# Selective scan: which engine makes the products with B, the first block's own order, and where five norms stand

## The chip, the cores and the metric

The kernel runs on one core of a Trainium2 chip. The metric is the device time of one execution in microseconds (us), as the median of several runs. A core has five engines that run their own queues in order and meet through semaphores: PE (TensorE, matrix products into PSUM), DVE (VectorE, elementwise work and scans), ACT (ScalarE, activation functions), POOL (GpSimd, elementwise work on SBUF alone here) and SP (SyncE, which issues the DMAs). PEld is PE's weight load.

## The reference

Four layers follow each other on two images of 128 channels and 64 x 64 pixels: attention, snake convolutions, convolution steps and, last, a selective scan in four directions (rows forwards and backwards, columns forwards and backwards). The change is in the last alone. For each direction, over a sequence of 4096 positions:

```python
dt = jax.nn.softplus(dt @ W_dt.T + b_dt)
A = -jnp.exp(A_log)
dA = jnp.exp(dt[..., None] * A)
dBu = dt[..., None] * Bm[:, :, None, :] * xh[..., None]
...
h = dA_t * h + dBu_t            # at each step t, for 256 channels x 16 states
...
y = jnp.einsum('lbdn,bln->bld', hs, Cm)
y = y + xh * Dp
y = y * jax.nn.silu(z)
return y @ W_out.T
```

The input is normalized over its channels first (mean, variance, scale). B and C come from xh by a matrix product; xh is a short convolution of the input followed by silu, and z another product.

## The kernel before

Layer 3 is one function, `layer3`. It works on 64 blocks: two images, four directions each, eight blocks of 512 positions per direction. A block has 8 groups of 4 tiles: two halves of the channels (`hf`) times four groups of four states (`ng`). A tile is 128 partitions (32 channels times 4 states) by 512 positions in fp32, so a group's `db` is 128 x 2048 and a block has 32 tiles.

A group k goes through these steps, each on one engine:

- `weights` (PE): the four rows of B of the group are spread over the partitions into PSUM, tile `pbc`, by a product with a selector.
- `db_dve` (DVE): the first n tiles of `db` = `pbc` times dt*x, where n is `ND[hf][ng]`. dt and dt*x lie spread over partitions in SBUF (`dd4`, one for each half).
- `db_pool` (POOL): the other 4 - n tiles, from a copy of B's rows in SBUF that a DMA has broadcast (`copies(.., "b", ..)`).
- `expo` (ACT): `da` = exp(dt*A) for one tile into PSUM, issued two tiles ahead of the scan; `da` has three buffers.
- `scan` (DVE): one scan per tile, in place in `db`, with the last column of the block before (`hl`) as its start. The first block of a direction starts at zero.
- `keep` (ACT): saves the last column of the group into `hl`.
- `cmul` (POOL): `db` times C's rows, in place; it may begin only when keep has read `db`.
- `sums` (PE): folds the four states and adds up over the groups into `py`.
- `gate` (DVE), `project` (PE) and `finish` (ACT): times silu(z), the output projection on top of the running image, and the copy back into it.

The scan layer stands in a manual schedule: the order of the calls in the code is the order in each engine's queue. The loop runs over k; within it `slot` is k modulo 8 and i the block. At slot s the loop issues the scans of group k, then `db_dve(k + 1)`, `db_pool(k + 1)` and `cmul(k - 1)`, and beside them one eighth of the preparation of block i + 1: its x product (slot 0), dt (slots 1 and 2), softplus, sums and the spreading through DRAM (`spread`, `spread_store`, `spread_load`), z (slot 4), and in slots 5 to 7 the convolution of block i + 2 with its silu. `transfers` issues the DMAs: spread_load is 8 transfers of 256 KB for each half, and B's and C's rows come by four transfers of 64 KB for each group. Silu needs another table than exp and ln, so each silu has a table load ahead and one behind it.

In before, `ND` is ((4, 2, 1, 4), (1, 4, 1, 4)): DVE makes 21 of a block's 32 tiles, in eight instructions, and POOL makes 11 in four. The pool `wk`, which holds `db`, has four buffers. `finish(i - 1)` is issued at the start of slot 6, so ACT does it ahead of slot 6's exponentials.

The norm of a row (here a row is one block of 512 positions) is `ln_mean` (PE), `ln_less` (DVE), `ln_square` (ACT), `ln_var` (PE), `ln_log` and `ln_root` (ACT), `ln_scale` (POOL) and `ln_store` (ACT). The mean and the variance use `da`'s PSUM buffers. In before all eight rows of the first image are normalized ahead of the loop, in a software pipeline with the preparation of block 0 and of block 1's convolution; the second image's eight rows are normalized one per block in blocks 22 to 29 (`next_norm`), at slots 0, 1, 3, 4 and 6. `turn` writes the column-wise copy of the first image in blocks 0 to 3, two rows in each.

## Time and profile before

| what | us |
|---|---|
| median of 3 runs (lowest to highest) | 5898.72 (5897.96 to 5899.47) |
| the profiled execution | 5899.89 |
| its span, first to last instruction | 5898.1 |
| scan layer: first DMA to first scan | 2453.30 to 2523.34 |
| scan layer: first scan to last scan's end | 2523.34 to 5883.5 |
| scan layer: last scan's end to the end | 14.6 |

The granted PE clock was 0.887 over the span. The page gives busy times over the whole span, in which three other layers fill the first 2453 us; for the scan layer they say little. The prediction therefore cuts the span into stages. In its listings a line of the timeline has start, length, engine, source line, operation, output and inputs, shape, count, and in brackets the idle time of the engine just before it and what ended it. A line of the groups has busy time and mean ns of one behind the count, and then the idle time before those instructions. Busy times of one instruction and the next overlap by some 0.1 us[...].

### The profile page before, as it was taken

The numbers are of one execution on the slowest core, as the hardware profiler recorded it, in microseconds if no ns is written. First come the engines' busy times: TensorE is split into PE (matmuls) and PEld (weight loads), VectorE is DVE, ScalarE is ACT, GpSimd is POOL, SyncE is SP. The second block draws the span as 40 slices with busy tenths as digits, with TensorE's granted clock in tenths as the row PEclk, the third lists the DMA queues.
The fourth block names the chain that finished last, engine by engine and source line by source line (L and its number), as shares of the span: only waits on it lengthen the run. The fifth ranks groups of instructions, "written<-read, shape, count | busy, mean of one in ns | idle before, by whom it ended". The sixth has DMA issues, their size and how long they took to land.

```text
span 5898.1 us, 58825 instructions
## 1 busy us (share of the span) xinstructions
PE 4930.2 (84%) x19238; PEld 1735.4 (29%) x19238; DVE 4452.2 (75%) x4266; ACT 3816.1 (65%) x5499; POOL 3632.0 (62%) x1200
## 2 busy tenths in 40 slices
PE   7999999989978779877777787878777787777776
PEld 3333333334434334322222222222222222222221
DVE  5333333355124688589999999999999999999998
ACT  4888888840035511377777777777777777777775
POOL 5111111100010021089999999999999999999999
PEclk8999999999988889988888888888888888888887
DMA  5000001030056200056655556555655566555564
GB/s 155 19 19 19 19 19 33 1 59 1 4 112 109 64 11 0 20 131 146 143 133 135 130 140 145 128 131 141 151 134 134 129 139 146 139 132 134 137 148 104
DMA packets 345402, 558.75 MB, mean 95 GB/s; under 512 B 70480, under 2 KB 125280, under 8 KB 344000
## 3 DMA queue, kind: packets, MB, share of 16 engines
q1 hardware_dynamic: 341952, 551.37, 40.4%
q10 hardware_dynamic: 3136, 3.56, 0.2%
q8 instruction: 152, 2.49, 0.2%
q14 instruction: 162, 1.33, 0.1%
HBM read 465.59 MB, written 89.13 MB: 94 GB/s over the span
## 4 chain that ended last, share of the span: by engine, by line
PE 52%; DVE 27%; POOL 9%; issue 5%; DMA 4%; ACT 2%; SPq 1%; DVEq 0%; POOLq 0%; ACTq 0%
DVE db L1429 18%; PE ps L287 10%; PE acc L303 8%; DVE db L1404 7%; POOL db L1439 6%; PE pm L1294 6%; PE m L1052 6%; PE m L566 5%; PE py L1447 2%; PE pm L1359 2%; PE pm L1466 2%; PE pm L1464 2%; PE acd L812 2%; DMA dx<-dd 1%; POOL dd L1367 1%
## 5 line engine op out<-in xcount | busy, mean ns | idle before, releaser
L1439 POOL TENSOR_TENSOR db<-db,c 128x2048 f32<-128x2048 f32 x512 | 2313.4, 4535 | 92.3 <-ACT hl L1434 82.6
L1429 DVE TENSOR_TENSOR_SCAN db<-da,hl,db 128x512 f32<-128x512 f32 x1792 | 2166.1, 1266 | 69.1 <-ACT da L1420 21.1
L1420 ACT ACTIVATE da<-dd,am 128x512 f32<-128x512 f32 x2048 | 1398.0, 689 | 727.5 <-DVE db L1429 701.2
L293 ACT ACTIVATE e<-ps 128x1024 f16<-128x1024 f32 x1024 | 992.2, 1021 | 135.6 <-PE ps L287 123.9
L1388 PE MATMUL pbc<-bc,sel 64*128 64x512 f32 x512 | 288.3, 563 | 695.4 <-DVE db L1404 695.3
L1413 POOL TENSOR_TENSOR db<-b,dd 128x1536 f32<-128x1536 f32 (+1 forms) x256 | 811.5, 3170 | 9.0 <-PE py L1447 4.4
L1404 DVE TENSOR_TENSOR db<-pbc,dd 128x2048 f32<-128x2048 f32 (+2 forms) x512 | 785.3, 1534 | 0.6 <-PE pbc L1388 0.6
L314 DVE RECIPROCAL rec<-acc 32x512 f32<-32x512 f32 x64 | 214.9, 3358 | 640.4 <-PE acc L303 640.4
L321 POOL TENSOR_TENSOR parts<-parts 32x512 f32<-32x512 f32 x64 | 80.5, 1257 | 976.2 <-DVE parts L320 976.2
L1447 PE MATMUL py<-db,fold 128*32 128x512 f32 x4096 | 639.7, 701 | 39.8 <-POOL db L1439 38.4
L287 PE MATMUL ps<-q,k 32*128 32x512 f32 x4096 | 656.4, 643 | 3.6 <-DVE flag L250 2.8
L303 PE MATMUL acc<-e,v 128*128 128x512 f16 x2048 | 532.1, 382 | 0.0
L1388 PEld LDWEIGHTS pbc<-bc,sel 64*128 64x128 f32 x512 | 105.8, 207 | 1184.1 <-DVE db L1404 1070.4
L1052 PE MATMUL m<-v,u 128*128 128x512 f32 x864 | 379.7, 603 | 49.3 <-DVE v L1021 49.3
L1359 PE MATMUL pm<-dd,ident 128*128 128x512 f32 x512 | 365.3, 852 | 4.6 <-ACT dd L1352 4.4
L1429 DVE TENSOR_TENSOR_SCAN db<-da,db 128x512 f32<-128x512 f32 x256 | 294.8, 1206 | 30.4 <-ACT da L1420 22.5
L303 PEld LDWEIGHTS <-v 128*128 128x128 bf16 x2048 | 158.5, 97 | 510.6 <-issue 389.4
L287 PEld LDWEIGHTS ps<-q,k 32*128 32x128 f32 x4096 | 229.4, 184 | 228.4 <-issue 169.6
L566 PE MATMUL m<-comb,w 64*128 64x512 f32 (+4 forms) x1296 | 269.9, 575 | 0.0
L686 POOL TENSOR_SCALAR yt<-y 32x512 f32<-32x512 f32 x8 | 18.2, 2272 | 379.8 <-DVE y L677 379.4
L1052 PEld LDWEIGHTS m<-v,u 128*128 128x128 f32 x864 | 166.9, 194 | 262.1 <-issue 216.1
L1294 PE MATMUL pm<-xn,wcs 128*128 128x512 f32 x512 | 237.1, 606 | 3.0 <-ACT z L1312 2.6
(317 smaller groups left out, 5991.2 us busy)
## 6 DMA issues: line engine op xcount, KB each, us to landing
dd<-dx SPq DMA_DIRECT2D x1024, 256.0 KB, 6.8
dx<-dd SPq DMA_DIRECT2D x128, 512.0 KB, 3.3
c<-bx SPq DMA_DIRECT2D x1024, 64.0 KB, 2.2
b<-bx SPq DMA_DIRECT2D x768, 64.0 KB, 3.3
hats<-pos SPq DMA_DIRECT2D x136, 256.0 KB, 9.8
q<-qd SPq DMA_DIRECT2D x32, 512.0 KB, 7.5
w<-in_conv0T SPq DMA_DIRECT2D x18, 288.0 KB, 8.8
q<-in_x SPq DMA_DIRECT2D x8, 512.0 KB, 6.3
```

Source lines behind the costliest of these rows:

```text
L287: nc.tensor.matmul(ps[:, i, :], k4[h % 2][rows, kb // 4, :], q4[h % 2][rows, qb * BLK : (qb + 1) * BLK], start=True, stop=True,)
L293: nc.scalar.activation(e[:, :n, :], ps[:, :n, :], AF.Exp)
L303: nc.tensor.matmul(acc, v3[b][:, kb, h, :], e[:, i, :], start=(kb == 0), stop=(kb == NS - 1))
L566: yield lambda q=q, dy=dy, src=src, i0=i0, i1=i1: nc.tensor.matmul(m[:, i0 * NF : i1 * NF], w[half, dy, q, x, :], src, start=(dy == KC and ...
L1052: nc.tensor.matmul(m[x], weights[j][:, dy, x, :], v[j][b][:, x, r0 : r0 + RP, :].rearrange("p r i -> p (r i)"), start=(dy == 0), stop=(dy ...
L1294: nc.tensor.matmul(pu, wcs[:, hf, s, :], window(blk, sgn * s), start=(s == 0), stop=(s == 3))
L1404: nc.vector.tensor_tensor(x["db"][:, :n, :], x.pop("pb").unsqueeze(1).to_broadcast([P, n, BLK]), S[i]["d4", hf][:, 1, :n, :], ALU.mult)
L1413: nc.gpsimd.tensor_tensor(x["db"][:, n:, :], S[i]["b", ng].unsqueeze(1).to_broadcast([P, 4 - n, BLK]), S[i]["d4", hf][:, 1, n:, :], ALU.mult)
L1420: nc.scalar.activation(da, S[i]["d4", hf][:, 0, q, :], AF.Exp, scale=am[:, hf, q, ng : ng + 1])
L1429: nc.vector.tensor_tensor_scan(d1, d0, d1, 0.0 if first else hl[:, hf, ng, q, :], ALU.mult, ALU.add)
L1439: nc.gpsimd.tensor_mul(v, v, S[i]["c", ng].unsqueeze(1).to_broadcast([P, 4, BLK]))
L1447: nc.tensor.matmul(S[i]["y", hf][32 * q : 32 * q + 32, :], fold, G[k]["db"][:, q, :], start=False, stop=(ng == NNG - 1),)
```

## The change

- `ND` becomes ((4, 0, 1, 4), (4, 4, 0, 4)). DVE still makes 21 tiles and POOL 11, but two groups (1 of the first half, 2 of the second: slots 1 and 6) are POOL's alone, and only one is shared. For the two, `weights` has no product and `db_dve` no instruction. Group 0 needs no copy of B now.
- `wk` gets a fifth buffer, and POOL's product is issued for group k + 2, behind `cmul(k - 1)`, instead of for k + 1 ahead of it. B's copies are issued one slot earlier (`ahead` 4 instead of 3).
- `finish(i - 1)` moves from the start of slot 6 to just before its fourth tile.
- Ahead of the loop only three rows are normalized, and block 0's preparation is written out in an order of its own. Rows 3 to 7 are normalized in blocks 0 to 4, in other buffers (`xc` and `sq`), as the second image's are; `turn` runs in blocks 1 to 4.

```diff
@@ -1127,7 +1127,7 @@
     nc, tc = g.nc, g.tc
     NJ = 4
 
-    ND = ((4, 2, 1, 4), (1, 4, 1, 4))
+    ND = ((4, 0, 1, 4), (4, 4, 0, 4))
     NNG = N_STATE // NJ
     HB = 1
     HC = 3
@@ -1174,7 +1174,7 @@
                     nc.tensor.transpose(pw[:, s * P : (s + 1) * P], ws, g.ident)
                 nc.vector.tensor_copy(wcs[:, hf].rearrange("p s o -> p (s o)"), pw)
         d4 = ctx.enter_context(tc.tile_pool(name="l3d4", bufs=2))
-        wk = ctx.enter_context(tc.tile_pool(name="l3wk", bufs=4))
+        wk = ctx.enter_context(tc.tile_pool(name="l3wk", bufs=5))
         up = ctx.enter_context(tc.tile_pool(name="l3u", bufs=2))
         ck = ctx.enter_context(tc.tile_pool(name="l3ck", bufs=2))
 
@@ -1205,6 +1205,7 @@
         xn = a.tile([P, HW + 2 * HB, HW], F32, name="xn")
         xt = a.tile([P, L + 2 * HC], F32, name="xt")
         N = {}
+        NFIRST = 3
 
 
         def ln_tile():
@@ -1216,7 +1217,7 @@
             nc.tensor.matmul(N[k, "mean"], onesm, interior(g, b, k * RB, RB), start=True, stop=True)
 
         def ln_less(b, k):
-            if b == 0:
+            if b == 0 and k < NFIRST:
 
                 t = wk.tile([P, 4, BLK], F32, name="db")
                 N[k, "xc"], N[k, "sq"] = t[:, 0, :], t[:, 1, :]
@@ -1384,9 +1385,12 @@
         def weights(k):
 
             i, hf, ng = groups[k]
+            G[k] = {}
+            if ND[hf][ng] == 0:
+                return
             pb = psb.tile([P, BLK], F32, name="pbc")
             nc.tensor.matmul(pb, sel[:, ng].rearrange("p j c -> p (j c)"), S[i]["bc"], start=True, stop=True)
-            G[k] = {"pb": pb}
+            G[k]["pb"] = pb
 
         def copies(i, x, ng):
 
@@ -1397,22 +1401,28 @@
             for j in range(NJ):
                 nc.sync.dma_start(t[32 * j : 32 * j + 32], S[i]["bx"][r0 + j].partition_broadcast(32))
 
+        def db_tile(k):
+            if "db" not in G[k]:
+                G[k]["db"] = wk.tile([P, 4, BLK], F32, name="db")
+            return G[k]["db"]
+
         def db_dve(k):
             i, hf, ng = groups[k]
-            x, n = G[k], ND[hf][ng]
-            x["db"] = wk.tile([P, 4, BLK], F32, name="db")
-            nc.vector.tensor_tensor(
-                x["db"][:, :n, :], x.pop("pb").unsqueeze(1).to_broadcast([P, n, BLK]), S[i]["d4", hf][:, 1, :n, :], ALU.mult
-            )
+            n = ND[hf][ng]
+            if n:
+                nc.vector.tensor_tensor(
+                    db_tile(k)[:, :n, :], G[k].pop("pb").unsqueeze(1).to_broadcast([P, n, BLK]),
+                    S[i]["d4", hf][:, 1, :n, :], ALU.mult,
+                )
 
         def db_pool(k):
             i, hf, ng = groups[k]
-            x, n = G[k], ND[hf][ng]
-            if n == 4:
-                return
-            nc.gpsimd.tensor_tensor(
-                x["db"][:, n:, :], S[i]["b", ng].unsqueeze(1).to_broadcast([P, 4 - n, BLK]), S[i]["d4", hf][:, 1, n:, :], ALU.mult
-            )
+            n = ND[hf][ng]
+            if n < 4:
+                nc.gpsimd.tensor_tensor(
+                    db_tile(k)[:, n:, :], S[i]["b", ng].unsqueeze(1).to_broadcast([P, 4 - n, BLK]),
+                    S[i]["d4", hf][:, 1, n:, :], ALU.mult,
+                )
 
         def expo(k, q):
             i, hf, ng = groups[k]
@@ -1516,7 +1526,7 @@
                     spread_store(i, 1)
             if slot == 0 and i - 1 < NBK:
                 spread_load(i - 1, 1)
-            for x, ahead in (("b", 3), ("c", 1)):
+            for x, ahead in (("b", 4), ("c", 1)):
                 j, ng = divmod(8 * (i - 1) + slot + ahead, 8)
                 if ng < NNG and 0 < j < NBK:
                     copies(j, x, ng)
@@ -1548,6 +1558,8 @@
 
         def next_norm(i):
 
+            if i < NBLK - NFIRST:
+                return 0, NFIRST + i
             b, k = divmod(i, 4 * NBLK)
             k -= 4 * NBLK - 2 - NBLK
             return (b + 1, k) if b + 1 < NB and 0 <= k < NBLK else None
@@ -1560,41 +1572,62 @@
             nc.vector.memset(xt[:, HC + L :], 0.0)
             nc.vector.memset(xn[:, HB - 1, HW - HC :], 0.0)
             nc.vector.memset(xn[:, HB + HW, :HC], 0.0)
-
-            for t in range(NBLK + 2):
-                slot = t - 2
-                if slot == 6:
-                    for k in range(2):
-                        weights(k)
-                    db_dve(0)
-                    db_pool(0)
-                if slot >= 0:
-                    front_pe(0, slot)
-                    front_act(0, slot)
-                    front_pool(0, slot)
-                if slot == 1:
-                    bc_store(0)
-                elif slot in (3, 4):
-                    spread_store(0, slot - 3)
-                    if slot == 3:
-                        spread_load(0, 0)
-                        copies(0, "b", 0)
-                        copies(0, "c", 0)
-                if t < NBLK:
-                    for part in (ln_mean, ln_less, ln_square):
-                        part(0, t)
-                if 0 <= t - 1 < NBLK:
-                    for part in (ln_var, ln_log, ln_root, ln_scale, ln_store):
-                        part(0, t - 1)
-                if t == 1:
-                    begin(0)
-                    conv(0, 1)
-                    conv_silu(0)
-            for ng in range(1, NNG):
+            units = [(k, q) for k in range(len(groups)) for q in range(4)]
+            AHEAD = 2
+
+            for k in range(NFIRST):
+                ln_mean(0, k)
+            for k in range(NFIRST):
+                ln_less(0, k)
+            ln_square(0, 0)
+            ln_var(0, 0)
+            ln_log(0, 0)
+            ln_root(0, 0)
+            ln_scale(0, 0)
+            ln_square(0, 1)
+            ln_store(0, 0)
+            begin(0)
+            conv(0, 1)
+            ln_var(0, 1)
+            ln_log(0, 1)
+            ln_root(0, 1)
+            ln_scale(0, 1)
+            conv_silu(0)
+            front_pe(0, 0)
+            front_act(0, 0)
+            bc_store(0)
+            front_pe(0, 1)
+            front_act(0, 1)
+            ln_store(0, 1)
+            sum_parts(0, 0)
+            sum_copy(0, 0)
+            spread(0, 0)
+            spread_store(0, 0)
+            spread_load(0, 0)
+            softplus(0, 1)
+            front_pe(0, 3)
+            front_act(0, 3)
+            spread(0, 1)
+            spread_store(0, 1)
+            for ng in range(NNG):
                 copies(0, "b", ng)
                 copies(0, "c", ng)
-            units = [(k, q) for k in range(len(groups)) for q in range(4)]
-            AHEAD = 2
+            for k in range(2):
+                weights(k)
+            db_dve(0)
+            db_pool(0)
+            front_pe(0, 4)
+            front_act(0, 4)
+            front_pe(0, 5)
+            front_pe(0, 6)
+            ln_square(0, 2)
+            ln_var(0, 2)
+            ln_log(0, 2)
+            ln_root(0, 2)
+            ln_scale(0, 2)
+            ln_store(0, 2)
+            front_act(0, 7)
+            db_pool(1)
             for u in range(AHEAD):
                 expo(*units[u])
             for k in range(len(groups) + 7):
@@ -1606,9 +1639,9 @@
                 if k + 2 < len(groups):
                     weights(k + 2)
                 norm = next_norm(i)
-                if slot == 6 and 1 <= i <= NBK:
-                    finish(i - 1)
                 for q in range(4):
+                    if slot == 6 and q == 3 and 1 <= i <= NBK:
+                        finish(i - 1)
                     if norm and slot == 3 and q == 3:
                         ln_log(*norm)
                     if 4 * k + q + AHEAD < len(units):
@@ -1630,9 +1663,10 @@
                     ln_less(*norm)
                 if more:
                     db_dve(k + 1)
-                    db_pool(k + 1)
                 if ended:
                     cmul(k - 1)
+                if k + 2 < len(groups):
+                    db_pool(k + 2)
 
                 if slot == 5 and 0 <= k - 2 < len(groups):
                     sums(k - 2)
@@ -1652,9 +1686,9 @@
                         ln_store(*norm)
                 if live:
 
-                    if slot == 6 and i % (4 * NBLK) < NBLK // 2:
+                    if slot == 6 and 0 < i % (4 * NBLK) <= NBLK // 2:
                         for n in range(2):
-                            turn(blocks[i][0], 2 * (i % (4 * NBLK)) + n)
+                            turn(blocks[i][0], 2 * (i % (4 * NBLK) - 1) + n)
 
                 if slot != 5 and 0 <= k - 2 < len(groups):
                     sums(k - 2)
```

## The prediction

> **What bounds the kernel now.** I read the busy time by stage first, then groups by shape in the selective scan, then one block's timeline on each engine, then every idle gap of VectorE (DVE). By stage (span, busy and count of PE, weight loads, DVE, ACT, POOL, then clock and DMA), the scan layer's start and its 64-block loop:
>
> ```profile
> 2453.30:2523.30 70.00, 54.13 (x107) 19.94 (x108) 15.78 (x36) 42.07 (x61) 17.98 (x12) 0.87 0.35 88
> 2578.00:5883.50 3305.50, 2568.46 (x7717) 783.18 (x7717) 3217.53 (x2650) 2387.67 (x3920) 3213.61 (x887) 0.84 0.58 136
> ```
>
> In the loop DVE (3217.53) and GpSimd, POOL (3213.61), are each busy 97% of 3305.5 us; in the 70 us before it DVE does almost nothing. The change touches only these two stages. Shapes in the loop:
>
> ```profile
> L1429 DVE TENSOR_TENSOR_SCAN db<-da,hl,db 128x512 f32<-128x512 f32 x1789 | 2162.6, 1266 | 69.0 <-ACT da L1420 21.1 <-DVE db L1404 0.9 <-ACT hl L1434 0.5
> L1404 DVE TENSOR_TENSOR db<-pbc,dd 128x2048 f32<-128x2048 f32 x251 | 569.1, 2267 | 0.0
> L1404 DVE TENSOR_TENSOR db<-pbc,dd 128x512 f32<-128x512 f32 x189 | 126.0, 666 | 0.0
> ...
> L1439 POOL TENSOR_TENSOR db<-db,c 128x2048 f32<-128x2048 f32 x504 | 2277.3, 4535 | 83.2 <-ACT hl L1434 73.4 <-DMA dd<-dx 9.5
> L1413 POOL TENSOR_TENSOR db<-b,dd 128x1536 f32<-128x1536 f32 x189 | 650.2, 3440 | 8.4 <-PE py L1447 3.7 <-DMA c<-bx 3.0 <-POOL db L1439 0.9
> ```
>
> Busy times of neighbours overlap, so I take pitches, start to next start, from a block's timeline (start, length, engine, line):
>
> ```profile
> 5218.03 0.67 DVE L1404 TENSOR_TENSOR db<-pbc,dd 128x512 f32<-128x512 f32 x1
> 5218.80 2.46 DVE L1429 TENSOR_TENSOR_SCAN db<-da,hl,db 128x512 f32<-128x512 f32 x2
> 5221.17 0.67 DVE L1456 TENSOR_TENSOR gt<-py,z 128x512 f32<-128x512 f32 x1
> 5221.75 2.45 DVE L1429 TENSOR_TENSOR_SCAN db<-da,hl,db 128x512 f32<-128x512 f32 x2
> 5224.12 2.27 DVE L1404 TENSOR_TENSOR db<-pbc,dd 128x2048 f32<-128x2048 f32 x1
> 5226.49 4.81 DVE L1429 TENSOR_TENSOR_SCAN db<-da,hl,db 128x512 f32<-128x512 f32 x4
> ...
> 5209.32 4.53 POOL L1439 TENSOR_TENSOR db<-db,c 128x2048 f32<-128x2048 f32 x1 [1.14 <-ACT hl L1434]
> 5213.80 3.43 POOL L1413 TENSOR_TENSOR db<-b,dd 128x1536 f32<-128x1536 f32 x1
> 5217.19 9.04 POOL L1439 TENSOR_TENSOR db<-db,c 128x2048 f32<-128x2048 f32 x2
> ```
>
> A product with B of n tiles costs DVE 0.77 (n=1), 1.31 (n=2) or 2.37 us (n=4) until the scan that waits for it starts; a scan 1.18; a gate 0.58. One block is 32 x 1.18 + 4 x 2.37 + 1.31 + 3 x 0.77 + 2 x 0.58 = 52.05 with no idle, and undisturbed blocks repeat every 52.08. POOL needs 8 x 4.49 + 3 x 3.40 + 2.33 + 2 x 1.23 = 50.9 and waits some 1.1. So DVE bounds, POOL is 1.2 us behind it. Gaps then add to the time; the two kinds, DVE's gap and ACT's wait that makes it:
>
> ```profile
> 3702.61 2.46 DVE L1429 TENSOR_TENSOR_SCAN db<-da,hl,db 128x512 f32<-128x512 f32 x2 [1.99 <-ACT da L1420]
> 3700.77 0.57 ACT L1340 CAST bc<-pm 32x512 fp32r<-32x512 f32 x1 [1.60 <-PE pm L1337]
> ...
> 4672.78 2.34 DVE L1429 TENSOR_TENSOR_SCAN db<-da,db 128x512 f32<-128x512 f32 x2 [2.27 <-ACT da L1420]
> 4671.03 1.22 ACT L1472 ACTIVATE xa<-pm,vecs 128x512 f32<-128x512 f32 x1 [4.98 <-PE pm L1466]
> ```
>
> The first is in a block that also normalizes a row, the second is finish() standing at the head of slot 6. All DVE gaps of 0.2 us or more after the first scan add to 35.7 us: 13.8 in the eight norm blocks (3702 to 4083), 21.9 elsewhere, mostly finish. The start ends like this:
>
> ```profile
> 2517.93 0.81 ACT L1252 ACTIVATE xn<-db,vecs 128x512 f32<-128x512 f32 x1 [1.37 <-POOL db L1243]
> 2518.75 1.28 ACT L1299 ACT_TABLE_LOAD   x1
> 2520.04 1.26 ACT L1299 ACTIVATE u<-pm,vecs 128x512 f32<-128x512 f32 x2
> ...
> 2523.34 4.57 DVE L1429 TENSOR_TENSOR_SCAN db<-da,db 128x512 f32<-128x512 f32 x4 [10.51 <-ACT da L1420]
> ```
>
> The first products were ready at 2512.8; the first scan waits for ACT, which works through the eighth norm and block 1's silu.
>
> **What the Trainium skill says.** GPSIMD Engine Reference, section 3.1, gives 4497 ns for a tensor_tensor of 2048 fp32 on GpSimd and 2293 on VectorE; this trace has 4535 and 2267, so I price a whole-group B product like the C product, 4.49 pitch. SBUF — State Buffer, section "SBUF: two separate sides", says that GpSimd locks out a VectorE operation only if that has two SBUF inputs or a two-port mode. Here da, pbc and py are in PSUM, so DVE's products and scans have one SBUF tensor each; the trace agrees (scans 1256 to 1287 ns beside a 97% busy POOL). I charge no contention. ScalarE: Activation LUTs, "What ACT_TABLE_LOAD costs", gives 1283 ns and a drain of 1380; the trace has 1.28 us and the next activation 0.01 later, so I use 1.28.
>
> **Part 1, the split.** 21 of 32 tiles per block stay with DVE, in six instructions (five of four tiles, one of one) in place of eight. DVE: 5 x 2.37 + 0.77 = 12.62 against 13.1, 0.47 less, period 51.58. POOL: 2 x 4.49 + 3.40 = 12.38 against 12.5, total 50.8. Groups 1 and 6 now lie wholly on POOL, so I walked the block in slots (slot s = the four scans of group s, then the product for s+1). DVE's scans begin at 0, 4.7, 10.2, 17.9, 25.0, 32.1, 36.8, 44.5. POOL may take a C product only when keep() has run on ACT, which stands behind ACT's block of other work in that slot. That gives POOL starts of 1.8, 9.7, 14.2, 18.8, 24.8, 35.0, 39.5, 43.9 for the C products and, behind them, B products ending at 9.7 (group 2, its tiles scanned from 11.4), 33.7 (group 6, scanned from 36.8) and 52.9 = 1.4 of the next block (group 1, scanned from 4.7). Margins of 1.7, 3.0 and 3.3 us; POOL waits 0.8. The fifth tile is what lets POOL work two groups ahead: group 6's product needs the tile of group 1, summed by PE near 23.7, and group 1's the tile of group 4, summed near 46.4, against 29.2 and 48.4 when POOL asks. Eight scans now follow each other in slots 0 and 1 with no product between; ACT has 3 x 1.18 = 3.5 us there from one exponential to the next needed after its extra 1.05 us, and needs 2.4. Two PE broadcasts and four 64 KB DMAs (0.43 us of SP each) per block go; neither engine bounds, nothing gained. Gain 64 x 0.47 = 30. Bounds: 0, if POOL takes the lead at the old period, to 34.
>
> **Part 2, finish() at slot 6, q = 3.** It waits where project is done (PE near 35.4, finish near 39.8). PE's second convolution needs the PSUM buffer that finish frees, so starts at 40.8, ends 44.5; its silu runs at 48.7, so that is free. Of 21.9 I keep 5: gain 17, bounds 8 and 21.
>
> **Part 3, norms.** Rows 3 to 7 of the first image move from the start into blocks 0 to 4. Each adds 0.58 to DVE, 1.23 to POOL, about 4 us to ACT and three PE jobs, covered but for DVE's. The 2 us gaps of norm blocks came from slot 3's short cover (a one-tile product, 0.77) for Ln, Exp and a wait on PE; that cover is now 2.37, 1.6 more, so 0.4 is left. A new squeeze: slot 0's subtraction now directly precedes scans without a product, within 0.2 of what ACT can do. Before: 8 x 0.58 + 13.8 = 18.4. After: 13 x (0.58 + 0.4) = 12.7. Gain 6; bounds minus 10 (2 us in each of 13) and 8.
>
> **Part 4, the start.** Until xd is copied (2476.7) nothing moves: the second row's work fits ACT's 2.5 us wait for PE. Then softplus follows delta at 2478.2 (before 2481.5) and ends 2480.6; PE sum 1.2, copy 0.56, POOL 1.27 and gaps give 2483.7; the store takes 2.85 until the load is issued, 2486.6 against 2498.07; the load landed 12.1 after issue, so 2498.7. That isn't the last thing. ACT: second softplus to 2484.8, rest copy after PE at 2489, z with two tables 3.7 to 2492.8. PE: block 1's convolution from 2491.2, 5.4 + 3.7 as before, 2500.3, and row 2's variance queued behind it, 2501.3. Then Ln, Exp, POOL, store as from 2515.21 to 2518.75, 3.54; silu with tables 3.87; exponential 0.7: first scan at 2509.4. Gain 14; bounds 5 (transfers crowd: SP's 24 copies are queued behind the load) and 21 (PE's convolution at its faster pace, and the load decides). B's product of group 1 follows POOL's norm product at about 2503.7 + 4.5, in time for 2514.
>
> **Sum.** Old loop 5883.5 - 2523.3 = 3360.2 = 56 x 52.05 + 8 x 50.13 (each direction's first block has scans of 1.12) + 18.4 + 21.9 + 4 unexplained. New: 56 x 51.58 + 8 x 49.66 + 12.7 + 5 + 4 = 3307.5. Loop 53 less, start 14 less, the 14.6 us tail unchanged: 67. The profiled execution has a span of 5898.1 and took 5899.89; it gives 5833. The median of the runs, 5898.72, lies 1.2 lower: 5832.
>
> **Rivals.** A, the sum: 5832, 0.64, own range 5816 to 5848. B, POOL becomes the bound: for it speak its 97% and only 0.8 us of slack, against it the walk's margins. Then the split's 30 and a few us of part 2 go: 5865, 0.17. C, the start follows the load, and gaps vanish: 21 at the start and 5 in the loop more, near 5818, 0.09. D, slower: in slot 4 POOL now has a C product, group 6's whole product and the spread, 10.2 us against DVE's 7.1. If POOL enters that slot more than 3.0 us later than walked, group 6 arrives late in all 64 blocks; break-even is 67/64 = 1.05 us later still. Late by 4.6, the 1.6 us stall costs 102 and the time is 5934; 0.10. That the change doesn't do what it says is excluded: after's instruction order shows both whole-group products on POOL and three norms ahead.
>
> About 0.2% (12 us) is what can be told from no change. Faster: A, C and most of B, 0.88; same 0.03; slower 0.09. The range reaches from C to B, 5814 to 5866; beyond it lie D and the edges of both, about 0.15.
>
> **What would show it.** First scan at 2509 of the span; undisturbed blocks repeating every 51.6; DVE's B products in two shapes only, 320 and 64; no 2 us ACT wait before L1472/L1474's lines; norm blocks with gaps under 0.5. Wrong if DVE waits for POOL's db at groups 1, 2 or 6, if the period stays 52.1, or if gaps in slots 0 to 2 name ACT da.

## The result, and the profile after

| | before | after |
|---|---|---|
| median of 4 runs (lowest to highest), us | 5899.1 (5897.96 to 5899.47) | 5853.32 (5851.95 to 5854.64) |
| the profiled execution, us | 5899.89 | 5851.95 |
| its span, us | 5898.1 | 5850.1 |

The ratio is 0.9923, with a 95% interval of 0.9906 to 0.994. The kernel is 46 us faster; the prediction said 67. The same subtraction in the two traces, all in us of the profiled executions:

| stage | before | predicted | after |
|---|---|---|---|
| beginning of the span to the scan layer's memset of the averaging matrix | 2453.3 | 2453.3 | 2452.0 |
| from there to the first scan | 70.0 | 56.1 | 63.2 |
| first scan to the last scan's end | 3360.2 | 3307.5 | 3320.5 |
| last scan's end to the end | 14.6 | 14.6 | 14.5 |

So two stages are slower than forecast: the start by 7 us and the loop by 13. The first two stages of the scan layer in the trace after, as a table by stage (window, its length, then busy time and count of PE, weight loads, DVE, ACT and POOL, the clock, the DMA share and GB/s):

```profile
2451.90:2515.10 63.20, 45.27 (x83) 16.32 (x83) 12.46 (x31) 29.36 (x41) 11.73 (x7) 0.80 0.34 87
2515.10:5835.60 3320.50, 2587.84 (x7723) 793.29 (x7723) 3254.04 (x2571) 2453.91 (x4009) 3254.02 (x841) 0.84 0.56 133
```

DVE and POOL are now busy for the same 3254 of 3320.5 us, 98% each: so hardly any slack is left on either (97% each before). The groups by shape in the loop after (busy time, mean ns of one, idle time before them):

```profile
L1449 POOL TENSOR_TENSOR db<-db,c 128x2048 f32<-128x2048 f32 x510 | 2301.3, 4534 | 58.6 <-ACT hl L1444 55.6 <-DMA dd<-dx 2.2 <-DMA c<-bx 0.7
L1439 DVE TENSOR_TENSOR_SCAN db<-da,hl,db 128x512 f32<-128x512 f32 x1792 | 2157.1, 1264 | 57.1 <-ACT da L1430 12.8 <-POOL db L1422 8.9 <-DVE db L1413 0.5
L1413 DVE TENSOR_TENSOR db<-pbc,dd 128x2048 f32<-128x2048 f32 x319 | 722.5, 2265 | 0.0
```

DVE's products have the whole-group shape 319 times in this window, as the new split wants, and the scan is as long as before (1264 against 1266 ns), although POOL now works beside it nearly all the time. What is new is the second name in the scans' idle time: POOL's product with B, 8.9 us. Before, POOL was not among the names in that row, and had 0.8 us in the row of the scans that start from zero.

An undisturbed block repeats after 51.57 us in the timeline after. The second fence is ACT's `finish` in between: it has no wait.

```profile
5150.09 7.16 DVE L1439 TENSOR_TENSOR_SCAN db<-da,hl,db 128x512 f32<-128x512 f32 x6
...
5201.66 7.16 DVE L1439 TENSOR_TENSOR_SCAN db<-da,hl,db 128x512 f32<-128x512 f32 x6
```

```profile
5157.91 0.58 ACT L1484 COPY xa<-pm 128x512 f32<-128x512 f32 x1
```

From here on, "gaps" are the idle times of DVE that stand in front of a scan and are longer than about 0.15 us, summed from the first scan to the last. Before: 35.7 us. After: 26.5, of which 15.7 name ACT's exponential, 10.3 POOL's product with B. All but 0.5 us of them lie in the thirteen blocks that normalize a row (0 to 4 and 22 to 29) or at the head of the block behind such a stretch.

The names need a second look, because a scan of a POOL tile waits for both engines. Three of the gaps that name ACT (3.4 us) stand in front of the second scan of group 2, whose own exponential, counted in order on ACT, had ended 3.5 us earlier. In block 2 it ended at 2629.83 and POOL's product at 2633.37, just ahead of the scan:

```profile
2629.87 3.50 POOL L1422 TENSOR_TENSOR db<-b,dd 128x1536 f32<-128x1536 f32 x1
...
2633.39 1.28 DVE L1439 TENSOR_TENSOR_SCAN db<-da,hl,db 128x512 f32<-128x512 f32 x1 [1.15 <-ACT da L1430]
```

Going by which input of each scan ended last, POOL makes 13.8 us of the gaps, and ACT's exponential 8.8 in slot 4 and 3.6 in slots 1 and 2. One block with a norm after, engine by engine:

```profile
3841.88 2.08 PE L1234 MATMUL da<-sq,onesm 128*128 128x512 f32 x2 [0.59 <-DVE db L1439]
...
3849.34 0.57 ACT L1341 CAST bc<-pm 32x512 fp32r<-32x512 f32 x1 [1.59 <-PE pm L1338]
...
3851.19 2.46 DVE L1439 TENSOR_TENSOR_SCAN db<-da,hl,db 128x512 f32<-128x512 f32 x2 [1.09 <-ACT da L1430]
...
3851.35 4.54 POOL L1449 TENSOR_TENSOR db<-db,c 128x2048 f32<-128x2048 f32 x1 [2.68 <-ACT hl L1444]
...
3885.22 3.48 POOL L1422 TENSOR_TENSOR db<-b,dd 128x1536 f32<-128x1536 f32 x1
...
3888.74 1.28 DVE L1439 TENSOR_TENSOR_SCAN db<-da,hl,db 128x512 f32<-128x512 f32 x1 [0.95 <-POOL db L1422]
```

Read it downwards. In slot 3 the row's variance (L1234) takes PE 2.08 us ahead of the sum and the rest projection, ACT's rest copy waits 1.59 us for PE, and the exponential queued behind it and the root is 1.09 us late for the third scan of slot 4. `keep` stands behind the same wait on ACT, so POOL's C product waits 2.68 us. At the end POOL's product for group 2 of the next block ends at 3888.70, and DVE's second scan of that group, the first that needs it, has waited 0.95 us.

The gaps of slot 1 come about in the same way one slot earlier. In slot 0 the row's mean (L1217) stands on PE ahead of the x product, and ACT's copy of xd waits for that product. In block 1 the exponential behind this copy is 0.78 us late:

```profile
2567.58 2.07 PE L1217 MATMUL da<-xa,onesm 128*128 128x512 f32 x2 [3.01 <-DVE db L1439]
...
2573.10 0.58 ACT L1325 COPY xd<-pm 72x512 f32<-72x512 f32 x1 [1.33 <-PE pm L1319]
```

The start after, again across engines:

```profile
2464.12 8.73 PE L1295 MATMUL pm<-xn,wcs 128*128 128x512 f32 x16
2472.69 1.02 PE L1234 MATMUL da<-db,onesm 128*128 128x512 f32 x2
...
2473.81 0.69 ACT L1238 ACTIVATE db<-da,cst 128x512 f32<-128x512 f32 x1 [9.85 <-PE da L1234]
...
2480.16 0.58 ACT L1325 COPY xd<-pm 72x512 f32<-72x512 f32 x1 [1.13 <-PE pm L1319]
...
2507.00 0.69 ACT L1238 ACTIVATE db<-da,cst 128x512 f32<-128x512 f32 x1 [5.29 <-PE da L1234]
...
2515.14 4.57 DVE L1439 TENSOR_TENSOR_SCAN db<-da,db 128x512 f32<-128x512 f32 x4 [7.47 <-ACT da L1430]
```

The second row's variance is queued behind the sixteen passes of block 0's convolution, and ACT, which works in order, waits 9.85 us for it with block 0's silu behind. The third row's variance stands in the same way behind block 1's convolution, and ACT waits 5.29 us.

### The profile page after: what moved, and what is told of

Its sections match the earlier page's. It is cut to its first block, busy times and chain, and to the rows that moved or that the text cites. A ratio compares the mean times of both kernels' runs of the same rounds, so it can differ in the third digit from the quotient of the medians.

```text
span 5850.1 us, 57552 instructions
## 1 busy us (share of the span) xinstructions
PE 4896.9 (84%) x19110; PEld 1729.6 (30%) x19110; DVE 4431.4 (76%) x4138; ACT 3827.0 (65%) x5499; POOL 3620.6 (62%) x1136
## 4 chain that ended last, share of the span: by engine, by line
DVE 49%; PE 39%; issue 4%; POOL 3%; ACT 2%; DMA 2%; SPq 1%; DVEq 0%; POOLq 0%; ACTq 0%
DVE db L1439 34%; DVE db L1413 11%; PE ps L287 11%; PE acc L303 8%; PE m L1052 6%; PE m L566 5%; PE acd L812 2%; POOL db L1422 1%; DVE gt L1466 1%; PE m L526 1%; POOL db L1449 1%; PE pf L775 1%; PE pc L663 1%; PE pm L1295 1%; DMA hats<-pos 1%
## 5 line engine op out<-in xcount | busy, mean ns | idle before, releaser
L1439 DVE TENSOR_TENSOR_SCAN db<-da,hl,db 128x512 f32<-128x512 f32 x1792 | 2157.1, 1264 | 57.1 <-ACT da L1430 12.8
L1457 PE MATMUL py<-db,fold 128*32 128x512 f32 x4096 | 613.8, 684 | 257.2 <-POOL db L1449 255.0
L1422 POOL TENSOR_TENSOR db<-b,dd 128x2048 f32<-128x2048 f32 (+1 forms) x192 | 799.9, 4166 | 0.0
L1413 DVE TENSOR_TENSOR db<-pbc,dd 128x2048 f32<-128x2048 f32 (+1 forms) x384 | 767.3, 1998 | 40.4 <-DMA dd<-dx 40.4
L1392 PE MATMUL pbc<-bc,sel 64*128 64x512 f32 x384 | 210.1, 547 | 153.5 <-DVE db L1413 152.5
L1319 PE MATMUL pm<-u,wxp 128*72 128x512 f32 x256 | 200.8, 931 | 156.1 <-ACT u L1300 156.1
L1457 PEld LDWEIGHTS py<-db,fold 128*32 128x32 f32 x4096 | 89.7, 114 | 644.6 <-POOL db L1449 398.7
L1295 PE MATMUL pm<-xt,wcs 128*128 128x512 f32 x512 | 235.0, 601 | 28.3 <-ACT xa L1484 17.7
```

The costliest lines, as they stand in the source:

```text
L1413: nc.vector.tensor_tensor(db_tile(k)[:, :n, :], G[k].pop("pb").unsqueeze(1).to_broadcast([P, n, BLK]), S[i]["d4", hf][:, 1, :n, :], ALU.mult,)
L1422: nc.gpsimd.tensor_tensor(db_tile(k)[:, n:, :], S[i]["b", ng].unsqueeze(1).to_broadcast([P, 4 - n, BLK]), S[i]["d4", hf][:, 1, n:, :], ALU ...
L1439: nc.vector.tensor_tensor_scan(d1, d0, d1, 0.0 if first else hl[:, hf, ng, q, :], ALU.mult, ALU.add)
L1457: nc.tensor.matmul(S[i]["y", hf][32 * q : 32 * q + 32, :], fold, G[k]["db"][:, q, :], start=False, stop=(ng == NNG - 1),)
```

## The experiments

Each run was timed beside the kernel before on the same chip (medians there 5900.27, 5899.47, 5900.3 and 5900.35 us in the four sets). Edits are against the changed kernel; the letters of theories and rivals are those of the text ahead of each result. The changed kernel itself was run a second time, beside later ones:

> The changed kernel itself beside the next two, so that they are compared on one chip: 5848 to 5856 under every theory.

It took 5854.57 us (5849.1 to 5856.6), ratio 0.9922 [0.9906, 0.9939]. Its profiled execution had the same start, 63.19 us, but gaps of 21.1 instead of 26.5 us. So the gaps of one kernel differ by 5 us between two executions, and smaller differences of gaps are not read below. Those that name POOL were 9.3 and 10.3, those that name ACT 11.4 and 15.7. By the inputs of the scans, POOL made 12.2 and 13.8, ACT 4.6 and 8.8 in slot 4, and 3.9 and 3.6 in slots 1 and 2.

**finish back at the head of slot 6.**

```diff
+                if slot == 6 and 1 <= i <= NBK:
+                    finish(i - 1)
                 for q in range(4):
-                    if slot == 6 and q == 3 and 1 <= i <= NBK:
-                        finish(i - 1)
```

> The changed kernel with finish() back at the head of slot 6, all else as changed. Theory F (the move of finish is worth what the prediction charged, 17 us): 5870 us, and the trace shows ACT waits of 2 us or more before finish's copies with DVE gaps behind them, 20 us or more in all. Rival G (the split and the fifth tile alone took these gaps, because PE is no longer held back by the B broadcast of every group and has project done before slot 6 begins): 5853 us within 4, and no such gaps.

5849.16 us (5844.92 to 5853.44), ratio 0.9914 [0.9898, 0.9931]; gaps 20.0. The move is worth nothing on top of the rest of the change. Finish still waits here at times, but no gap of DVE stands behind it. Its longest wait on ACT in this kernel's loop, in the timeline:

```profile
3748.92 1.13 ACT L1484 COPY xa<-pm 128x512 f32<-128x512 f32 x1 [1.32 <-PE pm L1476]
```

Before, the sixteen finishes that add the bias (L1472) waited 46.4 us together, up to 4.98 in one. The two traces show why this is gone: before, PE ended the last sums ahead of the projection 0.5 us after the exponential that ACT does just before finish began (4665.87 and 4665.36 us); in this kernel they end 3.4 us ahead of it (4681.38 and 4684.75). Over all 64 blocks the medians are 0.9 us ahead of it before and 4.5 us ahead of it here. What fits is that POOL now makes the C product ahead of the B product, so that the sums come earlier against slot 6; which of the fifth tile, the order two groups ahead and the split is needed for it was not tried apart, so this stays a reading.

**The old split, in two forms.** The first has DVE's 21 tiles in eight instructions in place of six, with the shared groups in slots 1, 2, 5 and 6:

```diff
-    ND = ((4, 0, 1, 4), (4, 4, 0, 4))
+    ND = ((4, 2, 1, 4), (4, 1, 1, 4))
```

> The changed kernel with a split in eight DVE products per block again, n = (4, 2, 1, 4) and (4, 1, 1, 4): 21 tiles for DVE as before, POOL's 11 in four instructions, all other parts as changed. Theory S (DVE's start-up per product is what the split saves): undisturbed blocks repeat every 52.05 us in place of 51.57, 64 x 0.47 = 30 us more, 5883. Rival P (POOL's order, not DVE's instruction count, sets the block): period stays within 0.1 of 51.57 and the time within 6 us of 5853.

5923.83 us (5923.19 to 5928.04), ratio 1.0041 [1.0026, 1.0055]: 70 us slower than the change, and slower than before. Neither theory had that. DVE's timeline shows it, here in one of 63 blocks:

```profile
5199.39 0.66 DVE L1413 TENSOR_TENSOR db<-pbc,dd 128x512 f32<-128x512 f32 x1
...
5203.46 2.46 DVE L1439 TENSOR_TENSOR_SCAN db<-da,hl,db 128x512 f32<-128x512 f32 x2 [0.84 <-ACT da L1430]
```

Here DVE makes one tile (0.66 us) where both other splits have a whole group (2.27). ACT uses that stretch for z's silu with two table loads, 3.7 us, and the exponential behind it comes 0.84 us late. Together these gaps are 54.5 us; the sum's 30 for the eight instructions come on top, and the gaps beside norms, 26 us in the changed kernel, shrink to 2.4. That is about 60 of the 70 us. So a product is not only DVE's work, it is ACT's cover, and where the long ones stand counts. This run tells nothing of the split's own price, and the second form has exactly the split of before:

```diff
-    ND = ((4, 0, 1, 4), (4, 4, 0, 4))
+    ND = ((4, 2, 1, 4), (1, 4, 1, 4))
...
-                res = ck.tile([P, BLK], F32, name="res", bufs=1)
+                res = ck.tile([P, BLK], F32, name="sq", bufs=1)
```

> Everything as changed, the fifth tile and the order two groups ahead included, but the products with B are shared out exactly as before: (4, 2, 1, 4) and (1, 4, 1, 4) tiles for VectorE. (The last image's result tile shares a buffer with the norms' tile to make room for the two B copies this needs.) Theory S (each block costs VectorE 0.47 us less under the new split, and nothing else of part 1 matters): undisturbed blocks repeat every 52.05, the time is 64 x 0.47 = 30 us above the changed kernel's 5853, near 5883. Rival P (the gain comes from GpSimd working two groups ahead): period at or below 51.7 and a time within 8 us of 5853. Rival C (a product of one tile in front of a slot leaves ACT too little cover, so the old split has stalls that the whole-group split avoids): gaps of VectorE that name ACT's exponential return in slots 1, 4 or 6 of undisturbed blocks, more than 0.3 us a block, and the time is above 5895.

5879.36 us (5872.95 to 5884.46), ratio 0.9964 [0.9949, 0.9978]. Gaps are 20.9, near the changed kernel's sum but made otherwise: none is POOL's, and 17.9 stand in slot 4 of the norm blocks, which has a one-tile product of DVE in front of it again. An undisturbed block repeats after 52.08 us in its timeline:

```profile
5151.18 2.46 DVE L1439 TENSOR_TENSOR_SCAN db<-da,hl,db 128x512 f32<-128x512 f32 x2
...
5203.26 2.46 DVE L1439 TENSOR_TENSOR_SCAN db<-da,hl,db 128x512 f32<-128x512 f32 x2
```

Theory S holds: with all else as changed the split is worth 5879.4 - 5854 = 25 us, against 64 x 0.47 = 30 on paper; rival C's gaps in undisturbed blocks did not come. In the loops of the traces it is 3345.0 against 3320.5 and 3313.8.

**The old start.** All eight rows ahead of the loop in the old pipeline, no norm in blocks 0 to 4, `turn` in blocks 0 to 3:

```diff
-            if b == 0 and k < NFIRST:
+            if b == 0:
...
-            if i < NBLK - NFIRST:
-                return 0, NFIRST + i
...
+            for t in range(NBLK + 2):
+                slot = t - 2
```

> The changed loop (split, fifth tile, finish at q = 3) behind the old start: all eight rows of the first image normalized ahead of the loop in the old pipeline, none in blocks 0 to 4. Theory N (read from the changed kernel's trace: the new start gains 6.8 us, the five norms in the loop cost 5 x 0.58 on DVE and 9.5 in gaps): this is 5 to 6 us faster than the changed kernel, 5847 to 5848. Rival O (the prediction's sizes: start 14, norms 1 us each): 9 us slower, 5862.

5849.15 us (5845.68 to 5851.29), ratio 0.991 [0.9893, 0.9926]. The start is 70.1 us, so the new start is worth 6.9. But the loop has five norms less and takes 3305.0, gaps 16.7. The start and the five norms together bring nothing, if they do not cost some us.

**No norms in the loop.** The normalization of rows 3 to 7 of the first image, for which ones stand in, and of all rows of the second is left out:

```diff
+            nc.vector.memset(xn[:, HB + NFIRST * RB : HB + HW, :], 1.0)
...
-                norm = next_norm(i)
+                norm = None
```

> The changed kernel without the 13 norms inside the loop (rows 3 to 7 of the first image and all of the second are not normalized; the first's are filled with ones ahead of the loop). Theory N (all gaps of 0.15 us or more in the loop, 27 us, are made by the norms): 27 + 13 x 0.58 = 34.6 us less, 5819, and DVE has under 3 us of such gaps. Rival T (the gaps come from the turns of the first image and the first block of each direction, which lie in the same blocks): only the 7.5 us of subtractions go, 5846, gaps stay.

5815.88 us (5814.14 to 5818.74), ratio 0.9856 [0.984, 0.9873]; gaps 1.4, loop 3282.1. The thirteen norms make all the gaps but these 1.4 us and cost the loop 38 us in one trace of the change and 32 in the other: 2.4 to 3.0 us each, where 0.58 is DVE's own subtraction.

**Which part of a norm.** First the variance out of PE's way:

```diff
-                    if norm and slot == 3 and q == 3:
+                    if norm and slot == 4 and q == 1:
                         ln_log(*norm)
+                    if norm and slot == 4 and q == 3:
+                        ln_root(*norm)
...
-                        elif slot == 3:
-                            ln_var(*norm)
...
                     elif slot == 3:
-                        ln_root(*norm)
+                        ln_var(*norm)
```

> As changed, but in the thirteen blocks that also normalize a row the variance's matmuls are issued at the end of slot 3, behind the sum and the rest projection, the logarithm in slot 4 at q = 1 and the root there at q = 3 (before: matmuls first in slot 3, logarithm at its q = 3, root at its end). Theory V (the variance standing ahead of the sum and the rest projection on PE makes ACT's 1.6 us wait at the rest copy, with it the 1.1 us gap in slot 4 and GpSimd's late start): the gap at slot 4 goes in all 13 blocks and the gaps of VectorE fall from 26.5 to about 10, time near 5837. Rival G (GpSimd's own extra 1.27 us is what makes groups 1 and 2 of the next block late): only the slot 4 gaps go, 13 x 1.1 = 14 at most, and those naming GpSimd's products stay at 10 us, time 5840 to 5846. Rival X (the work is only moved: in slot 4 it meets z's silu and its table loads): gaps stay at 22 us or more, time within 5 us of 5853.

5844.7 us (5842.85 to 5849.05), ratio 0.9907 [0.989, 0.9923]. The gaps that name ACT fall to 5.0, those that name POOL stay at 10.3, loop 3309.4: as rival G said. None is left in slot 4; of ACT's, 4.4 stand in slots 1 and 2. The run moves ACT's logarithm and root out of slot 3 as well, and the rest copy still waits up to 2.63 us for PE in seven of the blocks, without a gap behind it. So it shows the variance and its ACT work as the cause in slot 3; their shares were not run apart.

Then GpSimd's product left out, the variance where the change has it:

```diff
-                    elif slot == 4:
-                        ln_scale(*norm)
```

> As changed, but GpSimd's product of a normalized row with its root is left out in the thirteen blocks (those rows enter the scan centred but not scaled, so the output is not the reference's). Theory V (the root is PE's order in slot 3; GpSimd is late because ACT's keep() is): the gaps that name ACT stay near 16 us and those that name GpSimd fall by less than half, time 5845 to 5851. Rival G (GpSimd's extra 1.27 us makes the lateness): the gaps that name GpSimd, 10.3 us, go, time near 5843.

5837.01 us (5831.91 to 5845.36), ratio 0.9894 [0.9877, 0.991]. The gaps that name POOL are gone (0.3; 1.0 by the inputs of the scans), those that name ACT are 9.8, 5.8 of them in slots 1 and 2. So two roots are shown by taking them away: the variance with its ACT work in slot 3, and POOL's own 1.27 us. A third, the mean ahead of the x product in slot 0, stands in both runs; it is read from the trace above.

**The start's variances ahead of the convolutions.**

```diff
             ln_square(0, 0)
             ln_var(0, 0)
+            ln_square(0, 1)
+            ln_var(0, 1)
...
             begin(0)
             conv(0, 1)
-            ln_var(0, 1)
-            ln_log(0, 1)
-            ln_root(0, 1)
-            ln_scale(0, 1)
             conv_silu(0)
...
             db_dve(0)
             db_pool(0)
-            front_pe(0, 4)
-            front_act(0, 4)
-            front_pe(0, 5)
-            front_pe(0, 6)
             ln_square(0, 2)
             ln_var(0, 2)
...
             ln_scale(0, 2)
+            front_pe(0, 4)
+            front_act(0, 4)
             ln_store(0, 2)
+            front_pe(0, 5)
+            front_pe(0, 6)
```

> As changed, but in the start the variances of rows 1 and 2 are issued on PE ahead of the convolutions that they stood behind: row 1's with its logarithm and root before block 0's convolution, row 2's before block 0's z projection. Theory Q (row 1's variance behind the 16 passes makes ACT wait 9.85 us and puts everything behind it 5 us late; row 2's, behind the next 16, ends the start): xd is copied near 2475 in place of 2480.2, block 1's silu follows the convolution directly, and the first scan stands 8 to 11 us earlier than 2515.1, time near 5843. Rival L (the load of the first dd lands when it does and then decides): xd earlier but the first scan less than 4 us earlier, time above 5849.

5842.04 us (5840.31 to 5843.3), ratio 0.99 [0.9883, 0.9916]; start 53.6 instead of 63.2 us. Theory Q holds; the load of dd was not what decided. DVE's first scan in its timeline, 3.59 us after the end of the first product (7.47 before this edit):

```profile
2507.60 4.57 DVE L1439 TENSOR_TENSOR_SCAN db<-da,db 128x512 f32<-128x512 f32 x4 [3.59 <-ACT da L1430]
```

**A norm without POOL.** The row is centred by a PE product with (identity minus averaging matrix) and squared from PSUM; later it is centred again, and DVE multiplies it from PSUM with the root. DVE has one instruction a row as before, POOL none:

```diff
+        def ln_centre(b, k):
+            N[k, "xm"] = ln_tile()
+            nc.tensor.matmul(N[k, "xm"], cen, interior(g, b, k * RB, RB), start=True, stop=True)
...
+            nc.scalar.activation(N[k, "sq"], N[k, "xm"], AF.Square)
...
+            nc.vector.tensor_mul(N[k, "xc"], N[k, "xm"], N[k, "sq"])
...
+                    if norm and q == 1 and slot in (3, 6):
+                        ln_centre(*norm)
```

> As changed, but the thirteen norms in the loop are computed in another form and order: PE multiplies the row by a centring matrix (identity minus the averaging matrix), ACT squares that straight from PSUM in slot 3, the variance's matmuls stand behind the rest projection at the end of slot 3, logarithm in slot 4, root in slot 5; in slot 6 PE centres the row again and VectorE multiplies it from PSUM with the root, which replaces VectorE's subtraction (still 0.58 us a block) and GpSimd's product (1.27 us a block, gone). The output is the same up to rounding. Theory T (two roots: PE's order in slot 3, and GpSimd's extra product, and nothing else): gaps of VectorE fall from 26.5 to 3 to 6 us, the loop is 3282 + 7.5 + 5 = 3294 in place of 3320, time near 5827. Rival M (the norm's ACT work has to stand somewhere and makes new gaps, wherever it is put): gaps stay above 13 us, time above 5838.

5852.95 us (5847.11 to 5853.92), ratio 0.9915 [0.9899, 0.9932]: no gain. The gaps that name POOL fell to 1.0, those that name ACT rose to 22.7. All of ACT's but one of 0.6 us stand in slot 4: those of slots 1 and 2 went with the mean, which this form does not have. That bears out the third root, though other work moved with it. The timeline shows that the new form had put the same stone in the same place:

```profile
3840.37 2.07 PE L1220 MATMUL da<-xa,cen 128*128 128x512 f32 x2 [2.06 <-DVE db L1454]
...
3845.89 0.59 ACT L1378 COPY dd<-pm 128x512 f32<-128x512 f32 x1 [2.23 <-PE pm L1375]
...
3849.55 2.68 DVE L1454 TENSOR_TENSOR_SCAN db<-da,hl,db 128x512 f32<-128x512 f32 x2 [2.14 <-ACT da L1445]
```

The centring product, which waits 2.06 us for one of the three `da` buffers and takes 2.07, now stands ahead of the sum in slot 3 where the variance stood, and the gap behind it is 2.06 to 2.41 us in nine of the thirteen blocks.

**Together.** The last form, the start of the variances' experiment, and the first three exponentials ahead of block 1's silu:

```diff
+            for u in range(3):
+                expo(*units[u])
             front_act(0, 7)
             db_pool(1)
-            for u in range(AHEAD):
-                expo(*units[u])
...
-                    if 4 * k + q + AHEAD < len(units):
...
+                    if 3 <= 4 * k + q + AHEAD < len(units):
                         expo(*units[4 * k + q + AHEAD])
```

> n_centre together with the start's variances ahead of the convolutions, and the first three exponentials issued ahead of block 1's silu with its two table loads. If the pieces add up: start 53.6 less 2 to 3.5 for the exponentials, loop 3294, together 37 to 40 us below the changed kernel, 5813 to 5817. Rival W (the earlier first scan only makes the first blocks wait for what the start still has to do): first scan as early as said, but gaps of 5 us or more in blocks 0 and 1, time near 5822.

5838.91 us (5835.1 to 5839.88), ratio 0.9895 [0.9879, 0.9912]. The time is above the 5813 to 5817 expected. The start gained more than expected, it is 49.5 us, and later gaps did not eat it; but the loop is 3317.6 with the slot 3 mistake in it. Then the one move, of the centring product and its square on ACT:

```diff
-                    if norm and slot == 3 and q == 3:
+                    if norm and slot == 2 and q == 2:
                         ln_square_of(*norm)
...
-                    if norm and q == 1 and slot in (3, 6):
+                    if norm and (slot, q) in ((2, 0), (6, 1)):
                         ln_centre(*norm)
```

> The last combination with one thing moved: the first centring matmul and its square stand in slot 2 (at q = 0 and q = 2) in place of slot 3 (q = 1 and q = 3), where PE's 2.07 us for it were in front of the sum and the rest projection. Theory V: that position alone made the 2.1 us gap in slot 4; it goes, no gap takes its place, gaps of VectorE fall from 25.0 to 3 to 7 us, the loop from 3317.6 to 3295 to 3299, time 5815 to 5820. Rival M (the norm's work on PE and ACT costs about 2 us a block wherever it stands): gaps stay above 15 us, time above 5830.

5821.81 us (5819.54 to 5826.14), ratio 0.9868 [0.9852, 0.9885]: 78 us faster than before and 32 faster than the change. The gaps in front of scans fall from 25.0 to 3.0, so theory V holds for the gaps, but the time and the loop, 3300.3, are a little above what was expected. The rest is a gap in front of another instruction, 7.2 us in seven of the thirteen blocks; one in DVE's timeline:

```profile
3892.64 0.69 DVE L1228 TENSOR_TENSOR xc<-da,sq 128x512 f32<-128x512 f32 x1 [1.21 <-PE da L1220]
```

The second centring stands behind the convolution on PE in slot 6 and is late for DVE. With the 3282.1 us of the loop without norms, 13 x 0.58 = 7.5 for DVE's instruction, 1.6 more at scans and these 7.2, the sum is 3298.4. Moving the second centring was not tried.

## Why the prediction was right in kind and wrong in size

- **Part 1, the split: right.** The period came out at 51.57 against 51.58, in the two shapes named; with the old split put back it is 52.08 and the time 25 us more, against 30 in the sum. No block has a gap that names POOL but those with a norm and the two that follow such a stretch, so the walk's margins held there, and rival D's late group 6 did not come.
- **Part 2, finish: gain right, edit wrong.** The gaps of slot 6 are 19.3 us before and none after, where the sum took 17 and kept 5; no finish in the changed kernel's loop waits. But the step that gave the gain to the move failed: with finish put back, nothing is lost. It set one edit against a wait of before without asking whether another edit, perhaps POOL's new order, removed that wait first.
- **Part 3, the norms: the step that failed.** "Covered but for DVE's" put POOL's 1.23 us for each norm at nothing. The sum's own figures say otherwise: 50.8 of work, 0.8 of waits and 1.23 for the product are 52.8 a block, against 51.58 + 0.58 = 52.16 for DVE, 0.7 short. Measured were 13.8 and 12.2 us in two executions, 1.1 and 0.9 for each norm, and 1.0 in all without the product. Rival B asked this of all 64 blocks alike, and it came true only beside the norms. The "new squeeze" in slots 0 and 1 was named and given no price; it is 3.6 and 3.9 us, and the trace puts it to PE's mean ahead of the x product. The term that had a price, 0.4 in slot 4, was of the right size: 8.8 and 4.6 us, 0.7 and 0.35 each. The longer cover did help there (with the one-tile product back, 17.9), but did not remove the cause. All gaps were 26.5 and 21.1, that is 2.0 and 1.6 for each norm in place of 0.4. The bound of minus 10 was a wrong sum: 2 us in each of 13 give 18.4 - 13 x 2.58 = minus 15. Measured were 18.4 - 38.4 = minus 20 and 18.4 - 31.7 = minus 13. Two of the prediction's signs of being wrong, DVE waiting for POOL at groups 1 and 2 and gaps in slots 0 to 2 that name ACT, appeared, beside the norms alone.
- **Part 4, the start: the step that failed.** "Until xd is copied (2476.7) nothing moves: the second row's work fits ACT's 2.5 us wait for PE" looked at ACT's idle time and not at what PE had queued ahead of the row's variance. The copy of xd ended at 2480.74, 4.0 us late on the clock and 5.4 when the 1.4 us by which this layer began earlier are counted. The gain was 7 instead of 14; with the variances ahead of the convolutions it is 16. From the third row's variance to the first scan the sum had 8.1 us, and 8.2 were measured (2506.96 to 2515.14).
- **The sum.** Loop: the part without norms and gaps was set 5 too high (3285.8; 3282.1 - 1.4 = 3280.7 measured). Gaps were set at 14.2 with those unexplained, and are 26.5 and another 5.7 that no listed gap holds; together plus 13. Start plus 7, the layers ahead minus 1: a span of 5831 + 19 = 5850. In time, 5853 lies outside the sum's own range of 5816 to 5848, to which the prediction gave 0.64. It lies inside the whole range, 5814 to 5866, only because that reaches to rival B, whose bound in all 64 blocks did not come: that part is luck.

## What to carry to other kernels

Work that is moved beside a full loop must be charged on every engine that it touches, in the blocks where it runs, against that engine's slack there; slack averaged over all blocks hides an overload in a fifth of them. In a fixed order longer cover on the consumer shortens a wait, and what stands ahead on the producer's queue makes it; an idle stretch of one engine can be filled only by work whose inputs the other engines' queues deliver within it. When several edits aim at one wait, undo them one at a time before giving one of them the credit. When a wait has two possible causes, compare the ends of both inputs, not the name alone.

## What was not expected of the hardware

The same averaging product (two passes, 128 x 512 fp32) took PE 1.02 us in the start and 2.08 us in the loop. The granted PE clock differs in the same proportion. Both stretches in the changed kernel, for these instructions alone (window, its length, busy time and count of PE and of its weight loads, the clock, the DMA share and GB/s):

```profile
2472.70:2473.70 1.00, 1.00 (x2) 0.18 (x1) 1.00 0.00 0
3841.88:3843.88 2.00, 2.00 (x2) 0.50 (x2) 0.50 0.00 0
```

It is not the wait ahead of it that tells the two apart: of the thirteen variances in this loop, eight ran at a clock of 0.50 and took 2.07 to 2.08 us behind waits of 0.54 to 0.89, and five at 0.71 to 1.00 and took 1.12 to 1.51 behind waits of 0.82 to 0.90. In the second execution five ran at 0.50. In both, gaps above 0.6 us in slot 4 stand only in blocks where the variance ran at 0.50. This fits the different gaps of the two executions; what sets the clock from one block to the next was not tried. A mean clock, 0.84 in the loop, hides a factor of two in the price of a single product.
